# Cross attention with layer norm: another order of all engines from the third tile on, and the two ends cut into column halves

## The chip, the cores and the metric

The kernel runs on one core of a Trainium2 chip. The core has five engines, each of which executes its own queue of instructions strictly in order: TensorE (PE, matrix products), VectorE (DVE), ScalarE (ACT), GpSimd (POOL) and SyncE (SP, which here only issues transfers). They wait for one another by semaphores. ACT and POOL issue a few transfers as well. The metric is the device time of one execution in microseconds. A lower number is better.

## The reference, cut to what matters

The input x has 4 sequences of 2048 rows of 512 columns; each sequence attends to 77 context rows of its own, with 16 heads of 32 columns. A boolean mask sets some of the 77 keys to minus infinity. The result is projected, x is added, and each row is normalised.

```python
q, k, v = heads(x @ wq), heads(ctx @ wk), heads(ctx @ wv)
scores = einsum('bhqd,bhkd->bhqk', q, k) / sqrt(32)
scores = where(mask, -inf, scores)
attn = einsum('bhqk,bhkd->bhqd', softmax(scores), v)   # heads joined again to 512 columns
out = attn @ wo + x
return (out - mean(out)) / sqrt(var(out) + 1e-5) * gamma + beta
```

All of it is float32.

## The kernel before

The 8192 rows of x are 64 tiles of 128 rows (numbers 0 to 63). Two tiles make a block (0 to 31), four tiles a group (0 to 15), and 16 tiles share one context. A float32 projection is made of three products of a rounded format: each operand is split into a high part (a cast on ACT) and a low part (a subtraction on DVE or POOL), and the three products high·high, high·low and low·high are summed in the same PSUM bank.

What one tile goes through, with the engine and the line of the code before:

- per group: `load_xT` loads x transposed (SP, L262), ACT casts it (L265), POOL subtracts (L269), and four visits of 12 matmuls of 128x512 (PE, L275) make the group's queries, which DVE copies out of PSUM (L289);
- per tile: the scores, 64 small products in four banks (PE, L405); DVE masks them and takes the maximum, in four quarters (L422); ACT exponentiates, in quarters too (L437); DVE takes the reciprocal of the sums (L447); POOL normalises (L452); DVE transposes (L473);
- per block: 12 transfers regroup the transposed weights (L484; `regroup_part`), issued by SP, ACT or POOL; the product with the values (PE, L498) fills two banks; ACT casts each bank (L527) and DVE subtracts (L531);
- per tile: SP loads the residual x (L539); the out-projection takes 12 matmuls of 128x512 (PE, L554); DVE adds the residual (L563) and takes the moments (L577, L578); POOL makes the reciprocal root per block (L583 to L586); ACT scales (L592), POOL multiplies by gamma and adds beta (L595, L598), and SP stores (L601).

The last tiles take a shorter way: the moments are taken from PSUM (L606, L608), POOL makes the root (L618, L619), DVE centres and multiplies by gamma in one instruction (L634), multiplies by the root and adds beta in another (L637), and SP stores. For tile 63 the residual goes into the PSUM bank by a product with the identity (L543, `resid`) ahead of its out-projection.

The order of all this is written out by hand. The string `ORDER` is a list of some 2100 words, and the kernel executes them one after the other. A word is a letter and a number: `S54` is the scores of tile 54, `T54.2` the third quarter of its maxima, `e54.2` of its exponentials, `r`, `n`, `t` its reciprocal, normalisation and transposition, `P23.5s` the regrouping transfer 5 of block 23 issued by SP (`a`: by ACT, `g`: by POOL), `V23` the product with the values of block 23, `a23.0` and `b23.0` the cast and the subtraction of its first bank, `Q59` and `q59` a visit of the query projection and its copy, `x21` the load of a residual, `O21` the out-projection, `+21` the addition of the residual, `s21` the moments, `k`, `f`, `)` scale, gain and shift, `w` the store, `g`, `i`, `j` load, cast and split of transposed x. Each word puts its instructions at the end of the queue of its engine. So the string sets, for each engine, in which order it works, and an instruction whose input is late holds everything behind it on the same engine. One exception: what the values' product of a block waits for is waited for already ahead of the scores that stand just before it on PE (`early_waits`).

Buffers are set by hand too: the strings `SLOTS` say which of a few slots each tile of data takes. There are 8 PSUM banks (`mm`), of which scores take four, so scores can start only as the banks of earlier work are read out; 3 score buffers in SBUF; 8 slots for residuals and outputs; 2 each for the regrouped weights, queries and the split operands.

At the start, the keys' projection (L299) begins when ACT has cast the first quarter of the keys' weights (L672). Ahead of it PE runs a few warming products.

Of the kernel before, what the change touches and what calls it, by code (L numbers as in the profile page):

```python
# [8 lines left out]
F32 = mybir.dt.float32  # L9
# [8 lines left out]
P = 128  # L18
# [26 lines left out]
LAST = 56  # L45

# [7 lines left out]
Z3.s P0.11s e4.3 e4.1 P0.9s n3 t3 P1.10s P1.4s P0.5s Q9 S6 T6.0 T6.2 T6.1 P1.2s P1.0s T6.3 P1.6s P1.8s P1.7s P1.5s
P1.9s P1.1s q9 Z1.s P1.11s r4 Q10 q10 e6.2 e6.1 j6 e6.3 D1 S5 T5.1 T5.3 e5.3 D2 T5.0 e5.0 Q8 q8 e6.0 j7 n4 t4 Z0.s
e5.1 S7 T7.3 e7.3 r6 T7.1 e7.1 P1.3s g8 Z5.s Z4.s T5.2 e5.2 T7.2 n6 Q14 q14 Q11 q11 Z16.s x4 g9 L1 Z13.s e7.2 Q13
Z15.s T7.0 t6 S9 T9.3 T9.0 e7.0 r7 n7 V1 T9.1 a1.0 b1.0 T9.2 r5 e9.3 x3 a1.1 b1.1 t7 P3.10s P3.1s x0 P3.11s P3.5s V0
a0.0 e9.2 b0.0 P3.6s i9 n5 t5 P2.5s O2 P3.3s P3.8s P3.9s e9.0 e9.1 S8 a0.1 T8.0 e8.0 T8.1 T8.2 e8.2 e8.1 b0.1 +2 T8.3
s2 P2.0s r9 O3 +3 s3 i8 P3.0s P3.2s O0 e8.3 j9 P3.7s P3.4s S10 T10.3 +0 T10.2 T10.0 q13 v1 k3 e10.3 r8 e10.0 T10.1
P2.2s g11 P2.11s n9 Z8.s Z14.s P2.9s P2.7s P2.6s e10.1 k2 O1 +1 s0 s1 P2.10s Q15 q15 n8 t8 Q12 P2.4s q12 S11 T11.1  # L60
T11.0 T11.2 =16.8 e10.2 v0 i11 =24.8 T11.3 r10 V3 a3.1 t9 P2.3s a3.0 b3.0 x6 P2.1s S12 T12.1 P2.8s b3.1 T12.2 x7 f2 j8
Q18 e11.0 e11.2 k1 n10 P4.4s g10 O7 f3 q18 P4.11s P4.10s )3 w3 j11 P4.9s g12 P4.5s )2 P4.6s P4.2s T12.0 S13 P4.3s V2
P4.0s T12.3 t10 e12.1 +7 s7 e11.3 e12.2 e11.1 r11 O6 T13.0 f1 P4.8s a2.1 n11 P4.7s b2.1 e12.0 P4.1s T13.2 T13.1 t11
P5.7s P5.4s +6 s6 v3 Z6.s P5.1s w2 x8 P5.10s i10 e13.0 a2.0 e12.3 e13.1 e13.2 Q19 q19 P5.3s S14 T14.3 T14.2 P5.6s r12
k0 P5.5s Q17 Q16 T14.1 b2.0 T14.0 T13.3 x5 P5.0s )1 w1 n12 P5.9s P5.11s P5.2s k6 e13.3 r13 S15 q17 q16 P5.8s e14.0
e14.2 t12 n13 T15.2 T15.0 k7 V4 a4.0 b4.0 T15.1 t13 P6.7s O4 +4 e15.2 j10 g13 f6 O5 +5 x9 Z9.s P6.6s P6.4s P6.8s f7 )7
e14.1 S16 T16.2 e14.3 r14 a4.1 b4.1 O9 T16.1 T15.3 P6.3s T16.0 P6.1s T16.3 e15.0 n14 t14 w7 e15.1 P6.9s S17 P6.5s
e15.3 r15 i12 T17.1 )6 P6.2s V5 T17.3 e16.0 e16.1 e16.2 T17.2 +9 e17.2 T17.0 s5 Z11.s P6.10s n15 f0 j12 t15 P6.0s
P7.10s P6.11s P7.6s P7.1s P7.9s w6 Q22 q22 e16.3 P7.7s s4 v2 a5.0 e17.1 s9 r16 i13 S18 P7.4s P7.8s P7.5s P7.11s )0 w0
O8 +8 s8 v4 T18.2 T18.3 T18.1 e17.3 e17.0 Q20 b5.0 x10 e18.3 r17 T18.0 e18.0 e18.2 q20 n16 t16 Q21 S19 T19.0 T19.3  # L70
T19.2 T19.1 q21 P7.0s P7.2s P7.3s k8 k5 a5.1 g14 j13 x11 Q23 Z10.s q23 x13 g15 n17 f5 e18.1 r18 e19.2 Q25 t17 q25 )5
k9 V6 b5.1 S20 a6.0 e19.1 b6.0 a6.1 e19.3 e19.0 O10 n18 t18 T20.2 f9 +10 b6.1 T20.1 T20.3 )9 O11 f8 P8.3s i14 j14 L2
P8.1s S21 T21.3 w5 )8 +11 T21.1 r19 n19 Z7.s P8.0s P8.10s P8.7s P8.5s w9 T21.0 s11 T20.0 P8.2s x12 P8.9s V7 k4 e20.3
T21.2 i15 j15 O13 t19 s10 S22 T22.2 +13 e20.2 a7.0 e21.0 e20.1 e20.0 r20 e21.2 v5 f4 n20 g16 b7.0 s13 P8.8s P8.11s
e22.2 O12 +12 P8.6s T22.3 P8.4s )4 Q27 a7.1 b7.1 T22.1 t20 P9.0s P9.5s q27 P9.6s P9.10s Z12.s w8 T22.0 s12 v6 P9.8s
Q24 q24 g17 e22.3 e21.1 e21.3 r21 n21 P9.3s x16 P9.4s Q26 q26 S23 T23.2 T23.1 T23.3 k10 f10 P9.11s P9.7s e22.1 e22.0
r22 )10 n22 P9.2s k13 e23.3 T23.0 t21 V8 a8.0 S24 T24.3 Q29 P9.1s e23.0 a8.1 e23.2 T24.0 e23.1 i16 T24.2 f13 )13 b8.0
b8.1 j16 O14 P9.9s t22 T24.1 x14 +14 s14 P10.7s P10.9s P10.4s k12 e24.0 e24.1 r23 S25 T25.1 T25.3 T25.2 T25.0 e24.3
i17 e25.1 e24.2 n23 O15 x15 +15 s15 k11 w4 O16 P10.5s v7 P10.8s P10.2s t23 S26 e25.0 T26.1 j17 T26.2 P10.0s x17 w13
P10.6s +16 T26.0 f11 P10.10s r24 P10.3s k14 n24 V9 a9.1 k15 f15 T26.3 e26.3 a9.0 e25.2 e25.3 e26.1 g18 P10.11s P10.1s  # L80
w10 P11.4s P11.11s x18 O17 +17 s17 P11.1s P11.2s q29 s16 t24 r25 Q28 q28 b9.0 b9.1 Q31 q31 Q30 q30 P11.10s S27 T27.2
P11.9s P11.6s P11.0s P11.5s f14 v8 x19 P11.7s P11.8s n25 )14 e26.2 e26.0 k16 r26 e27.2 n26 T27.0 T27.1 k17 f16 )16 V10
a10.0 e27.1 a10.1 f17 )15 T27.3 e27.3 t25 S28 P11.3s g19 T28.3 T28.2 b10.1 t26 T28.1 P12.0s P12.5s O19 P12.9s P12.2s
P12.6s e28.3 O18 +18 s18 w16 +19 b10.0 Q33 q33 w14 )17 )11 w15 e27.0 r27 T28.0 n27 i19 j19 i18 e28.1 S29 T29.1 e29.1
P12.7s e28.0 V11 T29.3 T29.0 P12.10s P12.11s x21 x20 P12.1s t27 P13.5s P13.10s P12.4s g20 O21 P12.8s P13.8s O20 a11.0
# [3 lines left out]
a12.0 t29 P14.5s L3 P14.7s f12 k21 f21 P14.2s x22 S32 T32.3 i20 g21 T32.2 b12.0 P14.9s a12.1 P14.1s P14.10s x24 )19
w19 P14.3s P14.0s T32.1 T32.0 k20 Q37 q37 t30 j20 f20 S33 T33.3 e31.2 O22 b12.1 O25 P14.6s P14.11s P14.8s x25 e32.1  # L90
T33.0 e32.0 T33.2 e31.0 e32.2 r31 e32.3 g23 )20 +23 s23 +22 V13 a13.0 T33.1 s22 n31 t31 P15.8s e33.2 P15.1s a13.1 i21
P14.4s P15.7s P15.3s S34 T34.3 T34.2 r32 )21 b13.1 T34.0 j21 w20 n32 v11 O24 +24 s24 T34.1 P15.0s P15.11s w21 P15.9s
P15.5s Q38 +25 q38 b13.0 s25 e33.1 e33.3 e33.0 r33 e34.2 k22 e34.1 )12 P15.2s v12 P15.6s Q39 q39 P15.10s t32 x27 n33
# [81 lines left out]
def xattn_layernorm(  # L175
# [386 lines left out]
    def residual(t):  # L562
        nc.vector.tensor_tensor(od[t], pos.pop(t), od[t], ALU.add)  # L563
# [237 lines left out]
```

## Time and profile before

| what | value |
|---|---|
| median of 3 runs | 510.7 us (510.17 to 511.24) |
| the profiled execution's own time | 511.24 us |
| its span | 509.4 us |
| mean granted clock of PE | 0.996 |
| busy PE | 500.0 us, 98% |
| busy ACT | 474.0 us, 93% |
| busy DVE | 460.0 us, 90% |
| busy POOL | 420.9 us, 83% |
| DMA traffic | 110.86 MB, mean 218 GB/s |

The span is what the profiler recorded from the first to the last instruction or transfer; 1.8 us of the profiled execution lie around it. Busy shares are over the whole span. The views of the profile name a line, an engine, an operation, its output and its inputs. "ACTq" and "SPq" are the sequencers that issue transfers. The bracket at the end of a timeline row gives how long the engine had been idle before the row, and what the idle time ended with.

### The profile page before, as it was taken

What the parts mean: (1) busy time and instruction counts of PE and PEld (TensorE: products, weight loads), DVE (VectorE), ACT (ScalarE), POOL (GpSimd) and SP (SyncE); (2) the same over time, 40 slices, a digit from 0 to 9 for tenths busy, and PEclk for the clock granted to TensorE, in tenths of its full rate; (3) what the DMA queues carried; (4) which work ended last, traced back from release to release, by engine and by line L of the source; (5) the groups of instructions that cost most, each with busy time, mean ns of one, the idle gap of its engine ahead of it and who ended that gap; (6) DMA issues with size and microseconds to landing.
All of it is one profiled execution on the core that took longest, in us unless ns stands there. A gap on an engine that the chain in (4) does not pass through costs nothing.

```text
span 509.4 us, 20326 instructions
## 1 busy us (share of the span) xinstructions
PE 500.0 (98%) x6831; PEld 383.1 (75%) x6831; DVE 460.0 (90%) x2539; ACT 474.0 (93%) x2248; POOL 420.9 (83%) x387
## 2 busy tenths in 40 slices
PE   8999999999999999999999999999999999999995
PEld 6987778777777777777777777777787677867773
DVE  5799989988999998988998998899898989899997
ACT  6699999999999999999999999999997999899851
POOL 3665655978899789978898988899997999989995
PEclk9999999999999999999999999999999999999998
DMA  8957757889788978577986897868679659887745
GB/s 305 396 215 175 164 157 203 215 212 241 185 264 243 230 190 230 157 205 187 252 241 206 199 246 234 236 167 237 196 206 262 190 171 260 231 210 215 189 156 226
DMA packets 58782, 110.86 MB, mean 218 GB/s; under 512 B 9462, under 2 KB 11278, under 8 KB 58678
## 3 DMA queue, kind: packets, MB, share of 16 engines
q1 hardware_dynamic: 54502, 101.30, 70.7%
q0 software_dynamic: 2496, 5.77, 4.2%
q10 hardware_dynamic: 1680, 2.49, 1.8%
q8 instruction: 54, 0.88, 0.8%
q14 instruction: 50, 0.41, 0.3%
HBM read 41.79 MB, written 16.78 MB: 115 GB/s over the span
## 4 chain that ended last, share of the span: by engine, by line
PE 80%; DMA 5%; DVE 5%; SPq 4%; ACT 2%; POOL 2%; issue 1%; ACTq 0%; DVEq 0%; POOLq 0%
PE pq L275 29%; PE po L554 29%; PE pa L498 9%; PE sc L405 9%; DMA out<-o 2%; SPq L484 2%; DMA PT<-B 2%; DVE B L473 2%; PE pv L326 2%; PE pk L299 1%; ACT pbuf L437 1%; SPq L539 1%; DVE pbuf L422 1%; PE pq L685 1%; DMA xtf<-xT 1%
## 5 line engine op out<-in xcount | busy, mean ns | idle before, releaser
L437 ACT ACTIVATE pbuf<-pbuf,nm 128x77 f32<-128x77 f32 x1024 | 352.9, 353 | 8.4 <-DVE q L289 3.4
L437 ACT ACTIVATION_READ_ACCUMULATOR pbuf<-pbuf,nm 128x1 f32 x1024 | 197.9, 193 | 0.0
L422 DVE CUSTOM_DVE_ANT_0 pbuf<-sc,mb 128x77 f32<-128x77 f32 x1024 | 170.4, 232 | 13.4 <-PE sc L405 11.2
L452 POOL TENSOR_TENSOR pbuf<-pbuf,ri 128x1232 f32<-128x1232 f32 x63 | 142.0, 2258 | 34.6 <-DVE ri L447 28.2
L554 PE MATMUL po<-woh,AH 128*128 128x512 f32 x256 | 104.6, 409 | 0.2 <-DVE AL L531 0.2
L275 PE MATMUL pq<-xth,wqh 128*128 128x512 f32 (+1 forms) x256 | 99.9, 390 | 0.2
L554 PE MATMUL po<-woh,AL 128*128 128x512 f32 x256 | 100.0, 391 | 0.0
L554 PE MATMUL po<-wol,AH 128*128 128x512 f32 x256 | 100.0, 390 | 0.0
L473 DVE STREAM_TRANSPOSE B<-pbuf 128x1280 f32<-128x1280 f32 x64 | 95.8, 1500 | 3.4 <-DMA out<-o 0.9
L275 PE MATMUL pq<-xtl,wqh 128*128 128x512 f32 (+1 forms) x256 | 98.1, 383 | 0.0
L275 PE MATMUL pq<-xth,wql 128*128 128x512 f32 (+1 forms) x256 | 98.1, 383 | 0.0
L422 DVE DVE_READ_ACCUMULATOR2_ANT nm<- 128x1 f32 x1024 | 84.6, 83 | 0.0
L595 POOL TENSOR_TENSOR o<-o,gam 128x512 f32<-128x512 f32 x56 | 72.1, 1292 | 3.9 <-ACT o L592 3.8
L598 POOL TENSOR_TENSOR o<-o,bet 128x512 f32<-128x512 f32 x56 | 71.9, 1291 | 1.6
L269 POOL TENSOR_TENSOR xtl<-xtf,xth 128x1024 fp32r<-128x1024 f32 x28 | 67.2, 2401 | 4.8 <-ACT xth L265 4.0
L405 PEld LDWEIGHTS sc<-kct,q 32*64 32x64 f32 x4096 | 51.9, 130 | 24.9 <-issue 12.6
L405 PE MATMUL sc<-kct,q 32*64 32x77 f32 x4096 | 62.2, 238 | 1.5 <-DVE nm L422 0.9
L554 PEld LDWEIGHTS po<-woh,AH 128*128 128x128 f32 x256 | 48.0, 187 | 16.4 <-issue 3.5
L498 PE MATMUL pa<-PT,vsb 96*32 96x256 f32 x992 | 59.7, 382 | 0.0
L275 PEld LDWEIGHTS pq<-xth,wqh 128*128 128x128 f32 x256 | 48.1, 188 | 11.4 <-issue 0.8
L554 PEld LDWEIGHTS po<-woh,AL 128*128 128x128 f32 x256 | 48.1, 188 | 10.9 <-DVE AL L531 0.4
L275 PEld LDWEIGHTS pq<-xth,wql 128*128 128x128 f32 x256 | 48.1, 188 | 9.6
(108 smaller groups left out, 638.2 us busy)
## 6 DMA issues: line engine op xcount, KB each, us to landing
PT<-B SPq DMA_DIRECT2D x330, 128.0 KB
xtf<-xT SPq DMA_DIRECT2D x28, 512.0 KB
o<-x SPq DMA_DIRECT2D x56, 256.0 KB
out<-o SPq DMA_DIRECT2D x56, 256.0 KB
PT<-B POOLq DMA_DIRECT2D x25, 128.0 KB, 4.7
PT<-B ACTq DMA_DIRECT2D x17, 128.0 KB
stage_a<-kin SPq DMA_DIRECT2D x4, 410.0 KB
xtf<-xT SPq DMA_DIRECT2D x4, 256.0 KB
```

The source lines that it names most:

```text
L269: return nc.gpsimd.tensor_tensor(l[:, c : c + 2], fx.pop((g, c)), xh[g][:, c : c + 2].bitcast(F32), ALU.subtract)
L275: nc.tensor.matmul(pq, w[:, c, m * P : (m + 1) * P], r[g][:, c, rs], start=(n == 0), stop=(n == 11))
L326: nc.tensor.matmul(pv[: rows.stop - rows.start], ctx_s[c][i][:, rows], v[c], start=(n == 0), stop=(n == 11))
L405: mm = nc.tensor.matmul(sc[j][r0 : r0 + SR, g * NK : (g + 1) * NK], qs[q, g, rs.start + r0 : rs.start + r0 + SR], kct[q, g, t // TPB, keys ...
L422: nc.vector.tensor_tensor_reduce(pb[:, h // 2, (h % 2) * NK : (h % 2 + 1) * NK], scs[t][j][:, g * NK : (g + 1) * NK], mb[:, t % TPB, keys_ ...
L437: nc.scalar.activation(pb[:, h // 2, (h % 2) * NK : (h % 2 + 1) * NK], pb[:, h // 2, (h % 2) * NK : (h % 2 + 1) * NK], AF.Exp, bias=nmax[t ...
L452: return nc.gpsimd.tensor_tensor(pv, pv, rv.to_broadcast((P, NP, 2, NK)), ALU.mult)
L473: nc.vector.transpose(bt.rearrange("p c q r -> p q c r"), pbuf[t % NPB].rearrange("p q (c r) -> p q c r", c=5),)
L498: nc.tensor.matmul(pas[b, g // 2][HD * j : HD * (j + 1), (g % 2) * BLK : (g % 2 + 1) * BLK], vsb[:, 2 * b // TPB, h % 2, HD * (h // 2) : H ...
L554: nc.tensor.matmul(pos[t], a[:, c, rs], w[:, c, :], start=(first and c == 0 and n == 0), stop=(c == NC_D - 1 and n == 2),)
L595: return nc.gpsimd.tensor_tensor(od[t], od[t], gam, ALU.mult)
L598: return nc.gpsimd.tensor_tensor(od[t], od[t], bet, ALU.add)
```

## The change

**The order.** From its 61st word on, `ORDER` is another permutation of the same words. The first 60 words, which reach to the start of the third tile, are the same, no word is added or dropped, and the words' meaning is the same but for the five below. The number of transfers that each queue issues is the same but for the last store. `SLOTS` is changed in the places that follow from the new order (PSUM banks, transposed x, outputs, and the small buffers of maxima, reciprocals, moments and roots). In the middle of the program two places may stand for the whole.

The first is PE and DVE around the scores of tiles 53 and 54. On PE before, the last matmuls of the query visit `Q59` (pq_14_3), the values' product of block 23 (pa_23), then the scores of tile 53 (sc_53):

```order
L275 MATMUL pq_14_3_7257<-xtl_14_6680,wqh_70 128x512
L275 MATMUL pq_14_3_7257<-xth_14_6664,wql_71 128x512
L498 MATMUL pa_23_0_7281<-PT_23_6835,vsb_75 32x256 x8
L498 MATMUL pa_23_1_7282<-PT_23_6835,vsb_75 32x256 x8
L405 MATMUL sc_53_0_7309<-kct_74,q_13_6672 64x77
L405 MATMUL sc_53_1_7310<-kct_74,q_13_6672 64x77
```

On PE after the change, the last two products of the scores of tile 53, the values' product, and the query visit:

```order
L406 MATMUL sc_53_2_7276<-kct_74,q_13_6740 64x77
L406 MATMUL sc_53_3_7277<-kct_74,q_13_6740 64x77
L499 MATMUL pa_23_0_7336<-PT_23_6820,vsb_75 32x256 x8
L499 MATMUL pa_23_1_7337<-PT_23_6820,vsb_75 32x256 x8
L276 MATMUL pq_14_3_7396<-xth_14_6510,wqh_70 128x512
L276 MATMUL pq_14_3_7396<-xtl_14_6526,wqh_70 128x512
```

The scores of tile 53 have moved ahead of the values' product and of the query visit; both before and after, the out-projection of tile 45 and then the scores of tile 54 come next. In words: `O43 O42 Q59 V23 S53 O45 S54` before, `O43 O42 S53 V23 Q59 O45 S54` after.

On DVE before, from the reciprocal of tile 51 to the first maxima of tile 53:

```order
L447 RECIPROCAL ri_51_7233<-sum_51_7122 128x16
L563 TENSOR_TENSOR o_42_6934<-po_42_7235,o_42_6934 128x512
L577 BN_STATS st_42_7254<-o_42_6934 128x6
L578 BN_AGGR mv_21_7217<-st_42_7254 128x2
L531 TENSOR_TENSOR AL_22_7135<-pa_22_1_7101,AH_22_7118 128x512
L473 STREAM_TRANSPOSE B_25_7272<-pbuf2_82 128x8x5x32
L289 COPY q_14_7302<-pq_14_3_7257 128x512
L473 STREAM_TRANSPOSE B_25_7272<-pbuf0_80 128x8x5x32
L422 ISA pbuf2_82,nm_53_7378<-sc_53_0_7309,mb_3_5869 128x77
```

The same stretch after, here from the transposition of tile 50:

```order
L474 STREAM_TRANSPOSE B_25_7234<-pbuf2_82 128x8x5x32
L532 TENSOR_TENSOR AL_22_7205<-pa_22_1_7111,AH_22_7128 128x512
L448 RECIPROCAL ri_51_7263<-sum_51_7094 128x16
L617 BN_STATS st_43_7267<-o_43_6939 128x6
L618 BN_AGGR mv_21_7269<-st_43_7267 128x2
L603 TENSOR_TENSOR o_42_6995<-po_42_7250,o_42_6995 128x512
L423 ISA pbuf2_82,nm_53_7310<-sc_53_0_7274,mb_3_6052 128x77
```

One transposition (tile 51, from pbuf0) and the copy of the query visit are now behind the first maxima of tile 53, the other transposition (tile 50) stands ahead of the reciprocal of tile 51. ACT has three transfers of block 24 (`P24.10a`, `P24.9a`, `P24.1a`) ahead of the last exponentials of tile 51, which that reciprocal needs.

The second place is SP around the load of the residual of tile 21. Before, from three stores:

```order
L601 DMA out<-o_16_3199 128x512
L601 DMA out<-o_14_3418 128x512
L601 DMA out<-o_15_3522 128x512
L484 DMA PT_12_3925<-B_12_3698 32x2x512 x3
L539 DMA o_21_4088<-x 128x512
L539 DMA o_20_4090<-x 128x512
L484 DMA PT_12_3925<-B_12_3698 32x2x512
```

After:

```order
L485 DMA PT_12_3941<-B_12_3742 32x2x512
L485 DMA PT_13_4138<-B_13_3939 32x2x512
L641 DMA out<-o_14_3202 128x512
L485 DMA PT_13_4138<-B_13_3939 32x2x512 x3
L540 DMA o_21_4331<-x 128x512
L641 DMA out<-o_16_3501 128x512
```

The load of tile 21's residual now stands behind the store of tile 14 and regrouping transfers of block 13; before it stood behind three regrouping transfers of block 12. The addition `+21` that reads it stood on DVE between the maxima of tile 30 (`T30.3 s20 +21 s21 T30.2`) and now stands between those of tile 31 (`T31.0 q33 +21 t29 T31.2`).

**The first keys' weights.** The cast of the first quarter of the keys' weights (128x512, ACT) is written as two casts of 256 columns.

**The last tile.** Its result is kept in two banks of 256 columns each. The words `X63`, `O63`, `s63`, `y63`, `z63` and `w63` now call the functions below: identity product and out-projection by half (12 matmuls of 128x256 each), the moments' statistics by half with one aggregation, centring and finish by half, and two stores, the first issued by SP and the second by ACT. `w63` does nothing.

```diff
+HALVES = slice(0, 256), slice(256, 512)
...
 ORDER = """
...
-P22.3s P22.6s P22.2s j28 t47 P23.8s P23.10s P23.2s b21.0 k39 e49.3 f39 )39 )37 n48 a21.1 P22.0s O40 e49.2 T49.0 e49.0
...
-e52.2 P24.8s V23 a23.0 n51 q59 t51 w40 P24.0s P24.4s P24.6s S53 O45 a23.1 )41 w41 v21 w38 e52.0 k42 P25.7a e52.3 T53.0
-P24.9a e53.0 P24.7s b23.1 k43 P25.8s P25.5s T53.3 e53.3 S54 T53.1 e53.1 T53.2 r52 e53.2 T54.2 T54.3 e54.3 T54.1 j30
...
+O43 +43 T51.0 w40 w38 P24.2s P24.9a P24.1a P24.0s P24.11s t50 b22.1 e51.0 e52.3 e52.0 P24.6s O42 r51 n51 P24.7s s43
++42 w39 P24.4s S53 T53.0 s42 v21 T53.3 e53.0 P24.3a x44 i30 V23 a23.0 j30 P24.5s t51 P25.6s P25.4s w35 P24.8s T53.2
+T53.1 e52.1 e53.1 r52 n52 b23.0 k43 f43 e53.3 k42 x47 P25.2s P25.8s Q59 O45 +45 s45 q59 x49 S54 T54.0 P25.0s T54.2
...
+    def last_half(n):
+        if n:
+            o_half(0)
+        tail[n] = bank(f"po_last_{n}")
+        nc.tensor.matmul(tail[n][:, :BLK], ident, od[NT - 1][:, HALVES[n]], start=True, stop=False)
+        if n:
+            o_half(1)
+
+    def o_half(k):
+        b, rs = NB * TPB // 2 - 1, slice(P, 2 * P)
+        ah, al = ahs[b], als[b]
+        for c in range(NC_D):
+            for n, (a, w) in enumerate(((ah, woh), (ah, wol), (al, woh))):
+                nc.tensor.matmul(
+                    tail[k][:, :BLK],
+                    a[:, c, rs],
+                    w[:, c, HALVES[k]],
+                    start=False,
+                    stop=(c == NC_D - 1 and n == 2),
+                )
+        nc.vector.bn_stats(st_last[:, k], tail[k][:, :BLK])
+
+    def last_moments():
+        t = NT - 1
+        mvs[t, 1] = tiny.tile([P, 4], F32, tag="mvt", bufs=len(ALONE), name=f"mvt_{t}")
+        nc.vector.bn_aggr(mvs[t, 1][:, :2], st_last)
+
+    def last_centre():
+        for v, cols in zip(tail, HALVES):
+            v = v[:, :BLK]
+            nc.vector.scalar_tensor_tensor(v, v, mvs[NT - 1, 1][:, 0:1], gam[:, cols], ALU.subtract, ALU.mult)
+
+    def last_finish():
+        t = NT - 1
+        o, r = od[t], mvs[t, 1][:, 2:3]
+        for v, cols, queue in zip(tail, HALVES, (nc.sync, nc.scalar)):
+            nc.vector.scalar_tensor_tensor(o[:, cols], v[:, :BLK], r, bet[:, cols], ALU.mult, ALU.add)
+            queue.dma_start(out[t * P : (t + 1) * P, cols], o[:, cols])
...
+    st_last, tail = tiny.tile([P, 2, 6], F32, tag="st_last", name="st_last"), [None, None]
...
         if c == 0:
             nc.vector.tensor_copy(ctx_s[c][0], ctx_f)
-            nc.scalar.copy(woh[:, c], wk_f)
+            for cols in HALVES:
+                nc.scalar.copy(woh[:, c, cols], wk_f[:, cols])
...
+    ends_last = {
+        "X63": lambda: last_half(0), "O63": lambda: last_half(1), "s63": last_moments, "y63": last_centre,
+        "z63": last_finish, "w63": lambda: None,
+    }
...
-        if op in "PU":
+        if word in ends_last:
+            ends_last[word]()
+        elif op in "PU":
```

More of the change, by code (lines that the diff above doesn't have):

```diff
@@ L54 @@
[L54 to L58, printed above, removed]
@@ L69 @@
[L69 to L73, printed above, removed]
@@ L89 @@
[L89 to L93, printed above, removed]
@@ L156 @@
     "xtl": "10101010101010101",
-    "xtf": "010101100101010101101010101010",
+    "xtf": "010101010101010110101010101010",
     "PT": "10100101010101010101010101010101011",
```

181 lines of the change are left out of this document (98 added, 83 removed).

## The prediction

> **What bounds the kernel now.** I read the page's totals first, then the windows of the span, then the chain of waits in order of time, and last the timelines of single engines where the chain leaves PE.
>
> ```profile
> span 509.4 us, 20326 instructions
> PE 500.0 (98%) x6831; PEld 383.1 (75%) x6831; DVE 460.0 (90%) x2539; ACT 474.0 (93%) x2248; POOL 420.9 (83%) x387
> PE 80%; DMA 5%; DVE 5%; SPq 4%; ACT 2%; POOL 2%; issue 1%; ACTq 0%; DVEq 0%; POOLq 0%
> 300.00:350.00 50.00, 50.00 (x707) 38.13 (x706) 44.60 (x263) 49.96 (x232) 46.45 (x38) 1.00 0.76 223
> 350.00:400.00 50.00, 49.77 (x671) 37.54 (x670) 44.23 (x242) 45.69 (x218) 44.83 (x38) 1.00 0.76 214
> 400.00:440.00 40.00, 38.71 (x571) 29.61 (x570) 37.57 (x231) 39.79 (x206) 37.55 (x41) 1.00 0.78 214
> ```
>
> The columns of a window are its length, then the busy time of PE, weight loads, DVE, ACT and POOL, the granted clock, the DMA share and GB/s. The reader is to see that PE is full: 50.00 of 50.00 us in a middle window, at a granted clock of 1.00. Only from 350 on does it lose something, 0.23 and 1.29 us. So reordering the other engines can save only where PE stands still, plus the two ends, which PE does not fill.
>
> How much does it stand still? Matmuls overlap, and a busy row hides short gaps. So I price PE's own work from the chain, where PE runs back to back, and compare the end.
>
> ```profile
> 12.03 5.75 PE pq L685 x48
> 17.78 2.88 PE pq L275 x24
> 100.88 1.86 PE pa L498 x32
> 102.74 2.96 PE po L554 x12
> 105.70 2.72 PE pq L275 x12
> 333.55 0.88 PE sc L405 x52
> 494.64 1.88 PE pa L513 x64
> 496.52 1.06 PE po L543 x2
> 497.58 5.72 PE po L554 x24
> ```
>
> (Start, length, what.) A visit of 12 big matmuls takes 2.72 us, and 2.96 right behind scores or a values' product; I call that 0.24 an entry. Scores take 0.88, a values' product 1.86. From 17.78 on PE has two double visits for group 0 (2 x 2.88), 60 more query visits, 64 out-projections and 3 value visits (127 x 2.72), 64 scores (x 0.88), 31 values' products (x 1.86), the two by tile (1.88), the identity product (1.06), and 58 entries in this order. The sum is 17.78 + 5.76 + 345.44 + 56.32 + 57.66 + 1.88 + 1.06 + 13.92 = 499.8. PE ends at 503.30 (497.58 + 5.72). So **3.5 us of stalls** lie in it, of which the windows show 1.5 (0.23 + 1.29). The stalls of the chain lie between 387 and 450; the largest is this:
>
> ```profile
> 402.05 0.34 PE L405 MATMUL sc<-kct,q 32*64 32x77 f32 x2
> ...
> 404.12 0.89 PE L405 MATMUL sc<-kct,q 32*64 32x77 f32 x58 [0.38 <-DVE nm L422]
> ```
>
> The scores of tile 54 start at 402.05 and end at 405.01 (404.12 + 0.89): 2.96 us instead of 0.88, a loss of 2.1. They wait for their banks, which DVE empties when it takes the maxima of tile 53 (L422). Why is DVE late?
>
> ```profile
> 396.40 0.25 DVE L447 RECIPROCAL ri<-sum 128x16 f32<-128x16 f32 x1 [0.97 <-ACT pbuf L437]
> 396.57 0.63 DVE L563 TENSOR_TENSOR o<-po,o 128x512 f32<-128x512 f32 x1
> 398.64 1.50 DVE L473 STREAM_TRANSPOSE B<-pbuf 128x1280 f32<-128x1280 f32 x1
> 400.07 0.65 DVE L289 COPY q<-pq 128x512 f32<-128x512 f32 x1
> 400.64 1.49 DVE L473 STREAM_TRANSPOSE B<-pbuf 128x1280 f32<-128x1280 f32 x1
> 402.06 0.20 DVE L422 CUSTOM_DVE_ANT_0 pbuf<-sc,mb 128x77 f32<-128x77 f32 x1
> L422 DVE CUSTOM_DVE_ANT_0 pbuf<-sc,mb 128x77 f32<-128x77 f32 x1024 | 170.4, 232 | 13.4 <-PE sc L405 11.2
> 385.19 0.36 ACT L437 ACTIVATE pbuf<-pbuf,nm 128x77 f32<-128x77 f32 x1 [3.40 <-DVE q L289]
> 443.48 0.36 ACT L437 ACTIVATE pbuf<-pbuf,nm 128x77 f32<-128x77 f32 x1 [1.31 <-DMA out<-o]
> ```
>
> DVE waits 0.97 us for tile 51's exponentials, then has two transpositions and a copy ahead of tile 53's first maximum at 402.06. ACT had stood idle for 3.40 us before 385.19; in its order the two regrouping transfers of block 23 that it issues itself (`P23.11a`, `P23.0a`) lie there. The second such hole, 1.31 us before 443.48, also at a transfer on ACT, delays tile 60's scores. I take the rest of the 3.5, 1.4 us, to be of this kind, in small pieces.
>
> **The change part by part.** The sum is made against the profiled execution, 511.24 us, whose span is 509.4; 1.8 us lie around it, which nothing here touches. The median of the runs is 510.7, 0.5 lower, and I carry my difference over to it.
>
> *Stall at tile 54.* Before, only one out-projection (2.96) stands between the scores of 53 and 54. Now the values' product, the query visit and the out-projection do: 1.86 + 2.96 + 2.72 = 7.54 us. In that time DVE has four quarters of maxima, the moments of tile 42 and one transposition. By the starts above a transposition occupies DVE for 1.43 (398.64 to 400.07) and a copy for 0.57 (400.07 to 400.64); the addition, the moments and one subtraction fill 396.57 to 398.64, of which I give the moments 0.8. A quarter of maxima is four operations, each of 170.4 / 1024 = 0.166 us busy, 0.67 in all. That is 2.7 + 0.8 + 1.43 = 4.9, and so 2.6 of cover. It is used up only if DVE again comes late, and that hangs on ACT, which now has three transfer issues ahead of tile 51's last exponentials. If ACT loses 3.40 there again, 0.6 of the stall comes back; if DVE is late by the cover and 2.1 more, all. Bounds 0 and -2.1, I take **-1.6**.
>
> *The other stalls, 1.4 us.* The new order is more even there too, but it keeps ACT's transfers, 21 as before. Bounds 0 and -1.4; I take **-0.5**, nearer to nothing, since the cause is not removed. If they go, nothing else is late next: PE's own work is the bound.
>
> *Entries.* One visit fewer comes right behind scores or a values' product (57 for 58): **-0.24**.
>
> *New small stalls.* A permutation of 2000 words brings tight places of its own: the scores of 18 follow those of 17 after one values' product (1.86 us), those of 47 follow 46 after one visit (2.96 us), and such a pair cost 2.1 above when DVE came late. DVE's slack there is not shown by any row of before. Bounds 0 and +2.1 for such a place; I take **+0.5** in all. The cover is that elsewhere scores are spread more evenly.
>
> *First keys' weights.*
>
> ```profile
> 4.24 0.62 ACT L672 CAST woh<-stage_a 128x512 fp32r<-128x512 f32 x1 [2.23 <-DMA stage_a<-kin]
> 4.91 0.84 PE L299 MATMUL pk<-ctx_h,woh 128*128 128x308 f32 x4 [0.62 <-ACT woh L672]
> L247 ACT CAST xth<-xtf 128x256 fp32r<-128x256 f32 x4 | 1.6, 402 | 0.0
> ```
>
> A cast of 256 columns takes 402 ns where this one takes 620, so PE starts 0.22 earlier; the second half comes some 0.36 later and may hold the third of the first four matmuls by a few hundredths. The subtraction that reads the whole weight comes 0.18 later, ahead of the ninth matmul. Bounds 0 and -0.22: **-0.15**. The chain is PE alone from 4.91 on, so it counts in full.
>
> *Last tile on PE.* The out-projection of 63 becomes 24 matmuls of 256 columns. In the row at 12.03, 48 of 256 columns take 5.75: 0.12 each, 2.88 for 24 where 2.72 stood. **+0.16**. The identity product's 1.06 is cut in two of about 0.53, one between the halves; no change.
>
> *Behind the last matmul.*
>
> ```profile
> 506.42 0.33 SPq L601 DMA_DIRECT2D out<-xtl  x1
> L248 DVE TENSOR_TENSOR xtl<-xtf,xth 128x256 fp32r<-128x256 f32 x4 | 1.7, 418 | 0.0
> L248 DVE TENSOR_TENSOR xtl<-xtf,xth 128x512 fp32r<-128x512 f32 x2 | 1.3, 683 | 0.0
> ```
>
> One half's statistics are taken while PE still works on the other: a DVE operation of 256 columns takes 418 where 512 take 683, so -0.27. Against that, two centrings and two finishes in place of one each pay a fixed part twice, 418 x 2 - 683 = 0.15 each: +0.30. So the second store is issued 0.03 later than the one store is now, and the first 0.39 earlier. From its issue at 506.42 to the end of the span the store now takes 3.0 us, for 256 KB; each half is 128 KB. No row shows a lone store of 128 KB: if only size counted it would save 1.5, if only the issue and the way counted nothing. Bounds 0 and -1.5; I take -0.3, near the second, since a transfer of 128 KB can take long too (the regrouping at 366.58, quoted below, 6.57). Together +0.03 - 0.3, **-0.3**.
>
> The Trainium skill, "DMA: Bandwidth & Descriptors", section "Anatomy of one DMA — SWDGE (gpsimd) path", gives a fixed 2.0 us and the bytes over 436 GB/s for another path of issue. By it the store would be 2.6 us and a half 2.3; the 3.0 here is somewhat longer, and the -0.3 agrees. [...]
>
> *Sum:* -1.6 - 0.5 - 0.24 + 0.5 - 0.15 + 0.16 - 0.3 = -2.1. The profiled execution would take 509.1, and the median **508.6 us**.
>
> **The rivals.**
>
> *B: the stalls only move.* ACT's transfer issues still stand ahead of exponentials, and ACT was idle 3.40 us at one. In the middle windows it is busy for 49.96 of 50.00, so it cannot catch up. Then 3.0 of the 3.5 us come back in other places, and the price is 510.7 - 0.5 (stalls) - 0.24 - 0.15 + 0.16 - 0.3 (entry, start, tail) + 0.5 (new stalls) = 510.2. For it: as many transfers on ACT as before. Against it: the longer gap ahead of tile 54.
>
> *C: slower, by a late residual load.* A program's order that is tight on DVE depends on SP too.
>
> ```profile
> 218.07 1.02 SPq L539 DMA_DIRECT2D o<-x  x2
> 229.41 0.67 DVE L563 TENSOR_TENSOR o<-po,o 128x512 f32<-128x512 f32 x1
> 366.58 6.57 DMA PT<-B
> 419.16 0.60 SPq L484
> 424.14 3.52 DMA out<-o
> L452 POOL TENSOR_TENSOR pbuf<-pbuf,ri 128x1232 f32<-128x1232 f32 x63 | 142.0, 2258 | 34.6 <-DVE ri L447 28.2
> L598 POOL TENSOR_TENSOR o<-o,bet 128x512 f32<-128x512 f32 x56 | 71.9, 1291 | 1.6
> ```
>
> Tile 21's residual was loaded 11.3 us ahead of its use. Now the load stands on SP behind the store of tile 14, which waits for POOL, and three regrouping issues, and its addition stands on DVE between the maxima of tile 31. From the scores of 30 (where POOL's shift of 14 stands) to the end of those of 31 PE has 0.88 + 2.96 + 2.72 + 0.88 = 7.4 us; taking off a shift (1.29), the store's issue (0.33 at 506.42) and three regrouping issues (0.60 each, as at 419.16), the load is issued some 3.9 us before that end, and lands 3.5 to 6.6 later (the rows 424.14 and 366.58): 0.4 before to 2.7 behind the scores. The addition's turn comes 2.6 behind them (three quarters of maxima and a copy), and DVE needs another 2.8 from it (0.67, 1.43, 0.67) ahead of the scores of 32, for which PE leaves 7.5 in all (two visits and a values' product). So a load that lands 4.7 behind the scores stalls nothing, and there are 2.0 to 5.1 to spare. It decides only if POOL is late by more: late by three normalisations (3 x 2.26 = 6.8) it stalls PE for 1.7 to 4.8, and with the four regrouping issues of block 13 held on SP by the same store, on which the next values' product waits, the upper half of that is likely: 3.7. The kernel would then take 508.6 + 3.7 = 512.3. For it: POOL is at 46.45 of 50.00 in a middle window. Against it: a POOL late by 6.8 would show somewhere in the old order, and PE there is full.
>
> **How the numbers follow.** The forecast has 0.55, with its own range from 506.9 (508.6 less the 1.4 of stalls not yet counted and another 0.3 from the store) to 509.7 (half of tile 54's gain and 0.3 of the other stalls lost). B has 0.27 and lies around 510.2, from 509.4 to 511.4. C has 0.18 and lies from 511.2 to 514. The range of 506.9 to 512.3 holds the first two and half of the third. Less than 0.2%, 1.0 us, can't be told from no change by a measurement of this kernel. Faster by more: nearly all of the forecast and a sixth of B, 0.58. The same: the rest of B with crumbs of the others, 0.24. Slower: 0.18, nearly all from C.
>
> **What would show it.** The gap-free sum of the new order is 499.8 - 0.24 + 0.16 - 0.15, so PE's last matmul ends at 499.6 plus the stalls (3.5 - 2.1 + 0.5 = 1.9): at 501.5 if I am right, at 503.1 if B is. The scores of tile 54 should take under 1.5 us from first to last matmul, with no L422 (now L423) wait in brackets; a wait for maxima at 18, 47 or elsewhere would be the new stalls. The first matmul of the keys should start at 4.7. From PE's last matmul to the end of the span, 6.1 us now (503.30 to 509.4), should be 5.8; 5.2 or less would say that half a store lands faster. An idle time of PE in the middle windows, 50.00 now, with DVE's addition waiting for "DMA o<-x", would be C. I would be wrong at the root if PE's visits themselves changed price, so that the sum no longer ends where the trace does.

## The result and the profile after

The changed kernel takes 508.08 us (median of 14 executions, 507.09 to 508.80) against 510.73 us (509.20 to 515.35) beside it on the same chip. The ratio is 0.9948, with a 95% interval of 0.9929 to 0.9966: faster by 0.3 to 0.7%. The forecast was 508.6.

The page's totals of the changed kernel, its chain by engine, and the two windows in which the kernel before lost time on PE (columns as before):

```profile
span 505.3 us, 20347 instructions
PE 498.6 (99%) x6845; PEld 383.9 (76%) x6845; DVE 461.0 (91%) x2542; ACT 474.1 (94%) x2249; POOL 421.3 (83%) x387
PE 91%; DVE 5%; DMA 2%; SPq 1%; POOL 1%; issue 0%; DVEq 0%
350.00:400.00 50.00, 50.00 (x673) 38.00 (x672) 47.56 (x265) 49.53 (x234) 46.83 (x42) 1.00 0.86 229
400.00:440.00 40.00, 40.00 (x582) 31.05 (x581) 37.60 (x231) 38.84 (x198) 37.36 (x37) 1.00 0.85 241
```

The profiled execution took 507.09 us, 4.2 less than the one profiled before. PE is now full in those windows too, and its share of the chain went from 80 to 91%. DVE, ACT and POOL are as busy as before, and PE's own work is the same to 0.1 us by the prices used below; PE's holes are gone. The chain around tiles 53 and 54 (start, length, what), then DVE's first maximum of 53, its reciprocal of tile 52, and one of the transfers that ACT issues here:

```profile
392.76 0.88 PE sc L406 x52
393.64 1.86 PE pa L499 x32
395.50 2.97 PE pq L276 x12
398.47 2.72 PE po L555 x12
401.19 0.88 PE sc L406 x53
...
395.95 0.23 DVE L423 CUSTOM_DVE_ANT_0 pbuf<-sc,mb 128x77 f32<-128x77 f32 x1
400.67 0.25 DVE L448 RECIPROCAL ri<-sum 128x16 f32<-128x16 f32 x1
386.30 0.61 ACTq L485 DMA_DIRECT2D PT<-B  x1
```

The scores of 53 end at 393.64, those of 54 start at 401.19: 7.55 us, as computed from the order. They take 0.88, so the stall of 2.1 us is gone. DVE begins the maxima at 395.95 and has left them at 400.67, when it goes on to tile 52's reciprocal. It came with 0.5 us to spare, not the 2.6 of the prediction, because it began 2.3 us after the scores: it was still busy with the addition of tile 42 and what stands ahead of it. ACT's issue here takes its 0.61 and no more, and ACT does not stand idle between 380 and 396.

The start and the end of the changed kernel:

```profile
4.63 1.06 PE L300 MATMUL pk<-ctx_h,woh 128*128 128x308 f32 x4
6.83 0.45 ACT L248 CAST ctx_h<-stage_a 128x308 fp32r<-128x308 f32 x1 [0.66 <-DMA stage_a<-kin]
11.99 5.75 PE pq L727 x48
17.74 2.88 PE pq L276 x24
...
499.39 0.28 PE L576 MATMUL po_last<-woh,AL 128*128 128x256 f32 x1
499.71 0.43 DVE L583 BATCH_NORM_STATS2 st_last<-po_last 128x6 f32<-128x256 f32 x1 [0.37 <-PE po_last L576]
500.30 0.70 DVE L677 SCALAR_TENSOR_TENSOR xtl<-po,mvt,bet 128x512 f32<-128x512 f32 x1
500.92 0.88 DVE L593 SCALAR_TENSOR_TENSOR po_last<-po_last,mvt,gam 128x256 f32<-128x256 f32 x2
502.20 0.33 SPq L600 DMA_DIRECT2D out<-xtl  x1
502.60 0.38 ACTq L600 DMA_DIRECT2D out<-xtl  x1
```

The first matmul starts 0.28 earlier (4.63 for 4.91), but the query projection behind the keys starts at 11.99 for 12.03; ACT waits 0.66 us for a later part of the keys' inputs. At the end PE finishes at 499.67, and the span goes on for 5.6 us, where it was 6.1.

### The profile page after: what moved, and what is told of

The parts are those of the page before. It is cut to its first block, busy times and chain, and to the rows that moved or that the text cites. A ratio compares the mean times of both kernels' runs of the same rounds, so it can differ in the third digit from the quotient of the medians.

```text
span 505.3 us, 20347 instructions
## 1 busy us (share of the span) xinstructions
PE 498.6 (99%) x6845; PEld 383.9 (76%) x6845; DVE 461.0 (91%) x2542; ACT 474.1 (94%) x2249; POOL 421.3 (83%) x387
## 4 chain that ended last, share of the span: by engine, by line
PE 91%; DVE 5%; DMA 2%; SPq 1%; POOL 1%; issue 0%; DVEq 0%
PE pq L276 35%; PE po L555 29%; PE sc L406 11%; PE pa L499 10%; PE pv L327 2%; DMA PT<-B 2%; PE pk L300 1%; PE pq L727 1%; DVE B L474 1%; SPq L485 1%; PE pw L689 1%; DVE po L674 1%; PE po_last L576 1%; DVE pbuf L423 1%; DVE xth L677 1%; DVE po L606 0%
## 5 line engine op out<-in xcount | busy, mean ns | idle before, releaser
L438 ACT ACTIVATION_READ_ACCUMULATOR pbuf<-pbuf,nm 128x1 f32 x1024 | 200.4, 196 | 0.0
L555 PE MATMUL po<-woh,AH 128*128 128x512 f32 x252 | 101.7, 404 | 0.0
L555 PE MATMUL po<-woh,AL 128*128 128x512 f32 x252 | 98.3, 390 | 0.1
L555 PE MATMUL po<-wol,AH 128*128 128x512 f32 x252 | 98.3, 390 | 0.0
L406 PE MATMUL sc<-kct,q 32*64 32x77 f32 x4096 | 60.7, 237 | 0.0
```

What stands on the lines that cost most here:

```text
L406: mm = nc.tensor.matmul(sc[j][r0 : r0 + SR, g * NK : (g + 1) * NK], qs[q, g, rs.start + r0 : rs.start + r0 + SR], kct[q, g, t // TPB, keys ...
L438: nc.scalar.activation(pb[:, h // 2, (h % 2) * NK : (h % 2 + 1) * NK], pb[:, h // 2, (h % 2) * NK : (h % 2 + 1) * NK], AF.Exp, bias=nmax[t ...
L555: nc.tensor.matmul(pos[t], a[:, c, rs], w[:, c, :], start=(first and c == 0 and n == 0), stop=(c == NC_D - 1 and n == 2),)
```

## The experiments

Three numbers are read from each profile: where the query projection's second pass starts (17.78 before, 17.74 after), where PE's last matmul ends, and where the span ends. PE's own work between the first two is known from the prices of the prediction (482.0 us for the old order with whole ends, 0.2 more with halves; 481.8 and 481.9 for the new one; one entry, 0.24, more where the scores of 53 are set back or early), so the rest is its stalls, to about 0.5 us, with what a lower granted clock costs in them. The table is worked out in this way from the profiled execution of each run. The median is over all executions: 14 for the first two rows, 6 for the late load, 12 for the others. The kernel before ran again beside each of three sets of runs. Its medians there were 511.31 (the changed kernel again, the two parts apart, the scores set back), 510.68 (two issues, scores early, the late load, the whole store) and 510.29 (the rest), so the ratios in the text compare better than the medians do.

| kernel | median us | second pass starts | PE ends | stalls of PE | from PE's end to the span's |
|---|---|---|---|---|---|
| before | 510.73 | 17.78 | 503.28 | 3.5 | 6.1 |
| after | 508.08 | 17.74 | 499.67 | 0.0 | 5.6 |
| after, again | 507.62 | 17.77 | 500.17 | 0.5 | 5.6 |
| after, a third time | 507.48 | 18.56 | 500.81 | 0.3 | 5.7 |
| new order, old ends | 507.80 | 17.67 | 499.35 | 0.0 | 6.1 |
| old order, new ends | 509.86 | 17.85 | 502.59 | 2.5 | 5.6 |
| new order, scores of 53 set back | 511.50 | 18.14 | 505.37 | 5.0 | 5.6 |
| old order, two issues from ACT to SP | 509.99 | 17.79 | 501.39 | 1.6 | 6.1 |
| old order, scores of 53 set early | 510.82 | 18.55 | 503.53 | 2.7 | 6.2 |
| old order, eleven issues from ACT to SP | 512.51 | 18.58 | 502.39 | 1.8 | 6.2 |
| old order, eleven issues and scores early | 511.15 | 18.10 | 502.63 | 2.3 | 6.2 |
| after, one load late | 514.76 | 17.93 | 507.31 | 7.4 | 5.7 |
| after, one whole store | 508.17 | 18.51 | 500.42 | 0.0 | 6.0 |
| after, finish of 62 earlier | 508.01 | 17.81 | 499.59 | 0.0 | 5.7 |

### The changed kernel again

No edit. Two more profiles, each beside other runs.

> The changed kernel once more, beside the others. Theory 'stalls': PE's gap-free sum ends at 499.6, and what a typical execution (508.1) has above the profiled one (507.1) are stalls of PE that come and go, so this profile shows PE stalls of 0.2 to 1.5 us between 100 and 495, and 508.1 as median. Rival 'clock': the difference between executions is the granted clock, PE has no stall and each visit is 0.2% longer.

> The changed kernel a third time, to stand beside the others on this chip: 507.6 to 508.1, span going on 5.6 us behind PE.

Medians of 507.62 (ratio 0.9932, interval 0.9907 to 0.9957) and 507.48 (0.9949, 0.9928 to 0.9970). PE's stalls are 0.5 and 0.3, so the theory holds at its lower end only (its median of 508.1 was 0.5 too high), and a typical execution has hardly more stalls than the first profiled one. What else differs is the start: in the third profile the second pass starts 0.8 later (18.56 for 17.74). The granted clock is 0.997 and 0.999, no reason for any of it.

### The two parts apart

```diff
 # new order, old ends: the kernel before with ORDER and SLOTS of the changed one
-        "5012367450123456702315467023616312047536420762403712056301425672015467154206701253467021534062571347"
+        "5012367450123456702315467023614372546310642574032165070153462705627345064723517024635120462314507614"
...
 # old order, new ends: the changed kernel with ORDER and SLOTS of the one before, one bank more
-        "3612074340523743067251430572616752140521376172035462014675"
+        "36120743405237430672514305726167521405213761720354620146754"
```

> The new order with the start and the last tile as they were before. Theory 'the order pays': 508.4, since the ends gave 0.47 behind PE and 0.04 at the start in the profiles and cost 0.16 on PE; PE's last matmul ends within 0.3 of 499.7, and the span goes on for 6.1 us. Rival 'the ends pay': half of the gain goes, 509.4 or more.

> The old order with both ends cut into halves. Theory 'the order pays': 510.4 (0.35 faster than before), the stall of 2 us at the scores of tile 54 still there. First matmul of the keys at 4.63, but the query projection not more than 0.1 earlier than 12.03, since the keys' inputs arrive when they did. Rival 'the ends pay': 509.4 or less.

Measured: 507.80 (0.9943, 0.9918 to 0.9968) with the order alone, 509.86 (1.0000, 0.9976 to 1.0024) with the ends alone. The order pays: alone it has the whole gain within the measurement. For the ends alone the times show no gain; the median is 1.45 below the one beside it, but the interval does not tell that from nothing. The old order keeps its stalls (2.5 of PE) whatever the ends are. The ends' 0.5 us behind PE shows in both profiles, 5.6 against 6.1. The start's halves give nothing: the second pass starts between 17.67 and 18.58 with the whole cast and between 17.74 and 18.56 with the halves.

### Where the scores of 53 stand

```diff
-P24.4s S53 T53.0 s42 v21 T53.3 e53.0 P24.3a x44 i30 V23 a23.0 j30
+P24.4s V23 Q59 S53 T53.0 s42 v21 T53.3 e53.0 P24.3a x44 i30 a23.0 j30
...
-P25.8s Q59 O45
+P25.8s O45
```

> The new order, only the values' product of block 23 and the query visit 59 set back ahead of the scores of tile 53 on PE, as they stood before; DVE and ACT as in the new order. Theory 'gap': DVE had 0.5 us to spare ahead of the scores of 54 in the new order, and its maxima of 53 can now begin only at 398.3 instead of 395.95, so the scores of 54 are stalled by 1.8 us: 509.9. Rival 'ACT hole': the stall of the old order came from ACT's idle 3.40 us, which is not in the new order, so nothing is stalled: 508.1 to 508.4.

Measured 511.50, 3.9 above the changed kernel beside it (507.62); 1.0006 of the kernel before (0.9977 to 1.0034). DVE's first maximum of 53, PE's timeline, then four windows of 2 us, with the granted clock third from the end:

```profile
400.52 0.24 DVE L423 CUSTOM_DVE_ANT_0 pbuf<-sc,mb 128x77 f32<-128x77 f32 x1 [2.46 <-PE sc L406]
403.38 0.35 PE L406 MATMUL sc<-kct,q 32*64 32x77 f32 x4
404.77 0.34 PE L406 MATMUL sc<-kct,q 32*64 32x77 f32 x2 [1.03 <-DVE nm L423]
405.40 1.23 PE L406 MATMUL sc<-kct,q 32*64 32x77 f32 x58 [0.29 <-DVE nm L423]
406.56 0.80 PE L555 MATMUL po<-woh,AH 128*128 128x512 f32 x1
407.15 0.63 PE L555 MATMUL po<-wol,AH 128*128 128x512 f32 x1
407.58 0.63 PE L555 MATMUL po<-woh,AL 128*128 128x512 f32 x1
...
404.00:406.00 2.00, 0.94 (x44) 0.79 (x51) 2.00 (x20) 2.00 (x13) 2.00 (x2) 0.90 0.27 62
406.00:408.00 2.00, 2.00 (x37) 1.55 (x27) 1.93 (x5) 2.00 (x10) 2.00 (x1) 0.50 0.89 260
408.00:410.00 2.00, 2.00 (x8) 1.63 (x7) 2.00 (x25) 2.00 (x10) 1.92 (x3) 0.75 0.62 186
410.00:412.00 2.00, 2.00 (x11) 1.64 (x10) 1.28 (x4) 2.00 (x13) 1.40 (x2) 1.00 0.82 211
```

The theory of the gap holds and its price was near for the wait: the scores of 54 go from 403.38 to 406.56, 3.2 us for 0.9, a stall of 2.3 where 1.8 was expected. The rival falls, because ACT has no such hole ahead of this place here and PE stalls all the same. But the loss was twice what was expected, and a part of the rest was in neither theory: behind the wait PE ran at half clock, 0.43 us from one matmul to the next where 0.227 is normal, for some 3 us. That is not all of it: the six of the twelve executions with a mean granted clock above 0.995 have a median of 510.9, still 3.3 above the changed kernel. Another stall of 0.9 us at 255 in this profile stays unexplained.

### What made DVE late in the old order

Two local edits of the old order, one for each reason that the prediction gave: ACT's hole ahead of 385, or DVE's work ahead of the maxima of 53.

```diff
 # two issues from ACT to SP
-P23.11a T50.1 P23.0a
+P23.11s T50.1 P23.0s
...
 # scores of 53 early (the banks of S53 and Q59 exchanged in part)
-s42 Q59 P24.1a b22.1 t50 i30 P24.11s e52.2 P24.8s V23 a23.0 n51 q59 t51 w40 P24.0s P24.4s P24.6s S53 O45
+s42 S53 Q59 P24.1a b22.1 t50 i30 P24.11s e52.2 P24.8s T53.0 T53.3 V23 a23.0 n51 q59 t51 w40 P24.0s P24.4s P24.6s O45
```

> The old order and ends, only the two regrouping transfers of block 23 that ACT issues in its hole of 3.40 us (parts 11 and 0) issued by SP instead, at the same places in the list. Theory 'ACT hole': ACT goes on, the reciprocal of tile 51 is not late, and the stall of 2 us at the scores of 54 goes: 508.7. Rival 'gap': DVE still has two transpositions and a copy ahead of the maxima of 53, one visit ahead of the scores of 54; at least half the stall stays: 509.7 or more.

> The old order and ends, only the scores of tile 53 ahead of the query visit 59 on PE, and two quarters of their maxima ahead of that visit's copy and of the transposition of tile 51 on DVE; ACT keeps its transfers and so its hole. Theory 'gap': the stall of 2 us goes, 508.9. Rival 'ACT hole': the late reciprocal holds DVE anyway, and less than 0.5 is won: 510.2 or more.

Without the two issues on ACT: 509.99 (0.9994, 0.9968 to 1.0019). In its profile (first fence: ACT, DVE, then PE) the scores of 54 go from 401.08 to 403.10, so the stall there is halved, from 2.1 to 1.1; PE's stalls go from 3.5 to 1.6. ACT's hole is not gone: it stands idle for 1.95 us, where it was 3.40, until the next transfer that it issues itself (`P23.5a`) is out (the bracket names POOL, and which of the two held it is not shown), and DVE's wait for the exponentials of tile 51 is 0.97 as before. That half of the stall stays is what the rival expected, but more than half of ACT's hole stayed with it. The median shows only 0.7 us, which the interval can't tell from nothing. With the scores early: 510.82 (1.0003, 0.9982 to 1.0025). The scores of 54 are stalled by 0.2 at most there, though DVE still waits 0.83 us for ACT ahead of tile 51's reciprocal (ACT's hole was 1.42 in this profile). But PE waits at 53 and at the visit behind it instead (second fence: 0.26 and 0.63 us), and the wait at tile 60's scores is larger (0.79 and 0.20 us where before had 0.20 alone).

```profile
383.85 0.70 ACTq L484 DMA_DIRECT2D PT<-B  x1
384.65 0.82 ACT L592 ACTIVATE o<-o,rn 128x512 f32<-128x512 f32 x1 [1.95 <-POOL o L595]
394.50 0.25 DVE L447 RECIPROCAL ri<-sum 128x16 f32<-128x16 f32 x1 [0.97 <-ACT pbuf L437]
401.08 0.75 PE L405 MATMUL sc<-kct,q 32*64 32x77 f32 x6
402.21 0.89 PE L405 MATMUL sc<-kct,q 32*64 32x77 f32 x58 [0.38 <-DVE nm L422]
```

```profile
394.11 0.91 PE L405 MATMUL sc<-kct,q 32*64 32x77 f32 x60 [0.26 <-DVE nm L422]
395.64 0.50 PE L275 MATMUL pq<-xth,wqh 128*128 128x512 f32 x1 [0.63 <-DVE o L563]
```

Neither theory alone is right. In the old order the stall at 54 needs both, a late ACT and a short gap: it goes with the longer gap here, and with ACT's hole in the next section, where all of ACT's issues are moved. In the new order the short gap is enough, since DVE's other work stands ahead of the maxima there and it then waits 2.46 us for the scores themselves. Most of the early scores' gain was given back on the spot.

### All of ACT's issues

```diff
 # blocks 23 to 26, eleven transfers, for example
-P26.2a q56 S56
+P26.2s q56 S56
```

The second kernel of this pair has the early scores of 53 as well.

> The old order and ends, with all eleven regrouping transfers of blocks 23 to 26 that ACT issues issued by SP instead, at the same places in the list. Theory 'ACT holes': the holes before 385 and 443 go, and with them the stalls of PE at 402 and 449; PE's last matmul at 500.5 to 501.2 in the profile, median 508.6. Rival 'moved': SP holds the loads and regroupings behind these issues and PE waits for them instead; 510 or more.

> The same, and also the scores of tile 53 and two quarters of their maxima set early as in the earlier local edit. Theory 'ACT holes': no more than the one before gives, 508.6, since the stall is gone already; the new wait of about 0.5 us at 394 costs. Theory 'gap': 0.5 to 1 faster than without the early scores.

Measured 512.51 (1.0032, 1.0000 to 1.0065) and 511.15 (1.0017, 0.9986 to 1.0049): no gain. In the first one's profile ACT has no hole ahead of 385, DVE does not wait for it ahead of tile 51's reciprocal, and the scores of 54 take 1.08 us: the stall of 2.1 is gone, as expected, while the gap is as short as before. So ACT's hole is one of its causes. The wait ahead of tile 60's scores has grown:

```profile
402.45 1.08 PE L405 MATMUL sc<-kct,q 32*64 32x77 f32 x64
440.76 0.36 ACT L437 ACTIVATE pbuf<-pbuf,nm 128x77 f32<-128x77 f32 x1 [2.56 <-DMA o<-x]
448.23 0.39 PE L405 MATMUL sc<-kct,q 32*64 32x77 f32 x16 [0.85 <-DVE q L289]
448.83 0.82 PE L405 MATMUL sc<-kct,q 32*64 32x77 f32 x48 [0.21 <-DVE q L289]
```

The expectation was badly set: ACT's second hole lies at issues of block 27, which this edit leaves on ACT, and it is 2.56 us here for 1.31 before. So the rival's form, a wait moved on, is what was seen at tile 60, though PE waits for DVE there; that the profile puts ACT's wait down to a load by SP (o<-x) would fit the rival. Over the whole profile PE's stalls are still fewer, 1.8 for 3.5, and yet the median is not better. Seven of its twelve executions show a mean granted clock of 0.995 or less and take 511.8 to 515.3; the other five take 508.4 to 510.6. Which transfer holds ACT at 440 is not shown.

### The load of tile 21's residual

```diff
-P13.9s x21 +21 w16 f18 n29 t29 T31.2 Q34 g20 P13.7s
+P13.9s w16 g20 P13.7s g21 P13.4s P13.11s P13.6s x21 +21 f18 n29 t29 T31.2 Q34
```

> The changed kernel, with the load of tile 21's residual 5.5 us later on SP, behind five regrouping issues, a store and two loads that stood behind it (issue at 235.6 instead of 230.1). By the working of the prediction's slower case a load that lands 4.7 us behind the scores of 31 (at 236.9) stalls nothing; this one lands 3.5 to 6.6 after 235.6, so PE stalls 2.2 to 5.3 us: 510.3 to 513.4. Rival 'late things are caught up': the scores of 32 wait, but PE's other waits later are taken up in it, and less than 1 us is lost.

In the changed kernel SP issues this load at 230.12 and DVE adds at 236.13 without waiting (first fence). With the load late (second fence: SP, DVE, then PE), the kernel takes 514.76 (1.0092, 1.0066 to 1.0118):

```profile
230.12 0.60 SPq L540 DMA_DIRECT2D o<-x  x1
236.13 0.68 DVE L603 TENSOR_TENSOR o<-po,o 128x512 f32<-128x512 f32 x1
```

```profile
234.70 0.61 SPq L540 DMA_DIRECT2D o<-x  x1
242.12 0.69 DVE L603 TENSOR_TENSOR o<-po,o 128x512 f32<-128x512 f32 x1 [5.75 <-DMA o<-x]
242.86 0.36 PE L406 MATMUL sc<-kct,q 32*64 32x77 f32 x2 [2.71 <-DVE o L603]
244.89 1.42 PE L406 MATMUL sc<-kct,q 32*64 32x77 f32 x58 [1.67 <-DVE nm L423]
246.84 0.63 PE L276 MATMUL pq<-xtl,wqh 128*128 128x512 f32 x1
250.09 0.40 PE L276 MATMUL pq<-xth,wqh 128*128 128x512 f32 x1
```

A load issued 4.6 us later cost 7 us. It landed 7.4 us after its issue (234.70 to 242.12), longer than the 6.6 that the prediction took as its worst. PE waited 4.4 us (2.71 + 1.67), inside the 2.2 to 5.3 expected; the other 2 to 3 are again the half clock, with which PE works from 244.9 to 249.9. Nothing was caught up later.

### The end

```diff
 # one whole store
         for v, cols, queue in zip(tail, HALVES, (nc.sync, nc.scalar)):
             nc.vector.scalar_tensor_tensor(o[:, cols], v[:, :BLK], r, bet[:, cols], ALU.mult, ALU.add)
-            queue.dma_start(out[t * P : (t + 1) * P, cols], o[:, cols])
+        nc.sync.dma_start(out[t * P : (t + 1) * P, :], o)
...
 # finish of 62 earlier (its word z62 is taken out)
         if n:
+            finish(NT - 2)
             o_half(1)
```

> The changed kernel, with one store of 256 KB by SP behind both half finishes of the last tile instead of two of 128 KB by two queues. Theory of the prediction: a half lands 0.3 us faster, so this is 0.3 slower than the changed kernel, with the end of the span 3.0 us behind the store's issue instead of 2.7. Rival 'serialized': two halves take as long as one whole, no difference.

> The changed kernel with the finish of tile 62 on DVE set between the statistics of the last tile's two halves instead of behind them (0.62 us off DVE's path behind PE, of which some 0.25 comes back as a later statistic). If DVE's chain sets the end: the span goes on for 5.2 us behind PE instead of 5.6, 0.4 faster. Rival 'POOL': the last root on POOL is not earlier, and 0.1 or less is won.

The whole store is issued at 503.35 and the span ends at 506.4, 3.0 us on; the last half in the changed kernel takes 2.7 (502.60 to 505.3; the same in its two other profiles). Every profile with one whole store has 3.0. The median is 508.17 (0.9957, 0.9942 to 0.9972), which can't be told from the changed kernel's; the 0.3 us are seen in the profiles alone. They are not a half that lands faster by itself: from the first half's issue the two take 3.1 us together (502.20 to 505.3), no less than one whole store, and what is won comes from the 0.4 us by which the first half leaves earlier.

```profile
503.35 0.33 SPq L600 DMA_DIRECT2D out<-xtl  x1
core 0 of [0], span 506.4 us
```

The earlier finish of 62 gives nothing, 508.01 (0.9957, 0.9935 to 0.9978) and 5.7 us behind PE. The second store is issued 2.79 us behind PE's end instead of 2.93, so DVE won 0.14 of the 0.4 expected, since the later statistic waits for that finish; and the store took 2.9 this time. None of these kernels is clearly faster than the changed one.

## Why the prediction was right, point by point

*The bound.* Right. PE's work was priced at 499.6 for its end without stalls, and PE ended at 499.67.

*The stall at 54.* Mechanism right, the term -1.6 was -2.1: the stall is wholly gone. The working held for the gap (7.55 for 7.54) and was off in the cover (0.5 us left, not 2.6): it counted DVE as free when the scores end, and DVE was 2.3 us behind. The reserve that the term kept back, ACT losing 3.40 again, did not come, though ACT has three issues in this stretch. (Against a cover of 2.6 such a loss would bring back 0.8, not the 0.6 of the working.) That this place rested on both causes is what the edits of the old order showed.

*The other stalls, -0.5.* Mis-sized: about -1.2 (1.4 before, 0.0 to 0.5 in the three profiles after, taken as 0.2). Which of the order's places did it was not tested one by one. *New small stalls, +0.5:* none were seen at 18 and 47; 0.22 us of idle PE at 494 in the second profile is the largest left in the three.

*Entries, -0.24, and PE's halves, +0.16.* Both are inside the 0.5 us by which the sum meets the trace.

*The start, -0.15.* Wrong: 0. The step "the chain is PE alone from 4.91 on, so it counts in full" failed. PE is in a row there, but ahead of it stand the keys' inputs that arrive by DMA, which ACT still waits for with the first cast done earlier; the next pass starts when it did. It varies by 0.8 to 0.9 us between profiles with either cast.

*The tail, -0.3.* It was -0.5 (6.1 to 5.6). The store's part is 0.3, as taken, by the head start of the first half. The Trainium skill, "DMA: Bandwidth & Descriptors", section "Anatomy of one DMA — SWDGE (gpsimd) path", has 0.3 for the difference of the two sizes on another path of issue, and the trace agrees in the difference (3.0 and 2.7), though no run has a half alone. The other 0.2 is DVE: the last store is issued 2.93 us behind PE and no longer 3.14, where the working said 0.03 later.

*The sum.* By the profiled executions the gain is 4.2 us, twice the forecast's 2.1, as the stalls went altogether. By the medians it is 2.65, since the profiled execution of before lay above its median and that of after below. That the point came so near has some luck in it: the stalls were under-counted, and the profile of before showed somewhat more of them than its median.

*The rivals.* B, stalls that move, is in part what the local edits of the old order did (new waits at 53 and longer ones at 60), and the full order did not. C did not come: in the changed kernel the load is issued 2.1 us ahead of the end of the scores of 31 (232.2), where 3.9 was worked out (its terms give 4.0), and still lands in time. Its way of pricing the wait held when the load was made late (4.4 us, 2.2 to 5.3 expected), but it left out the half clock; with it the load cost 7 us.

## What to carry to other kernels

Price the bound engine's own work from its shortest back-to-back rows and compare the sum with where it ends: the difference is all that an order can win, and here it was won to the last half microsecond. None of the four local edits of the old order was faster clear of its interval, though each had fewer stalls of PE in its profile than the kernel before (1.6 to 2.7 for 3.5; the old order with new ends has 2.5): they left waits or made new ones, and in some executions the clock fell. The whole new order had the gain; that it is the wider gaps between scores that do it is shown at tile 54 alone. And a wait of the matrix engine of about two microseconds can cost more than itself, so an order is worth more by the long stalls that it rules out than by the median of its stalls.

## What the runs showed of the hardware

With the scores of 53 set back, PE stood idle for 1.03 and 0.29 us with two small products between, and the granted clock was 0.50 from 405.6 to 409.0. With the late load it waited 2.71 and 1.67 us, and the clock was 0.50 from 243.1 to 249.9. The kernel before, in its profile, waited 0.49, 0.20 and 0.38 us with four such products between, and kept its full clock. How long a wait it takes can be read behind the last matmul, where PE has nothing more to do: in the fourteen profiles the granted clock falls to 0.50 between 2.0 and 5.3 us after PE's end (2.2 in the kernel before, 3.8 in the changed one, 5.3 with the scores of 53 early). So a wait of two microseconds is enough at times, and one of five is not at others. The Trainium skill, "TensorE: Matmul & The Clock Gate", section "What's actually happening", says that the clock falls after at least one idle window of about 3.4 us whose place is free-running; here a shorter wait, with two products in it, was enough; that it depends on the execution agrees.

This is also seen from outside. The fall behind the end alone takes the mean granted clock to 0.996 in the profile of the kernel before; a lower mean says that the clock fell elsewhere too. Of 95 executions of the kernel before that ran beside the experiments (four above 515.9 us are left out), 20 have a mean granted clock of 0.995 or less, with a median of 512.9 us; the other 75 have 510.2. None of the 38 executions of the changed kernel is so low (0.996 at least), and they lie within 506.8 and 509.0. That these 20 lost their clock at the stalls near 402 and 449 is likely but not shown: no such execution of that kernel was profiled.
